# Attention scores from bf16 part stacks, or from float32 operands on row strips of TensorE, in a four-layer gated cross-attention kernel

## The chip, the cores and the metric

The kernel runs on one core of a Trainium2 chip. Its engines work side by side and meet at semaphores: TensorE (PE in the profile; its weight loads are listed apart as PEld), VectorE (DVE), ScalarE (ACT), GpSimd (POOL) and SyncE (SP), which here only issues DMAs. ACT and POOL issue DMAs too. TensorE writes to PSUM, of which the kernel uses eight banks of 128x512 float32; everything else lies in SBUF or in DRAM. The metric is the device time of one execution in microseconds; the median of several runs is compared.

## The reference

Eight batch elements of 256 tokens with 256 features pass four layers. Each layer adds a gated cross-attention and then a gated feed-forward block:

```python
x = x + jnp.tanh(g_xattn[l]) * xattn_l(_layernorm(x), ctx_1024, ...)
x = x + jnp.tanh(g_ffn[l]) * ffn_l(_layernorm(x), ...)
```

Attention has 16 heads of 16 features. Of one layer, with projections and biases (layer 0 has none, its queries, keys and values are the normalised x and the context themselves, and it has a mask over the keys):

```python
scores = jnp.einsum('bqhd,bkhd->bhqk', q, k) / jnp.sqrt(16)
scores = jnp.where(mask == 0, -1e9, scores)          # layer 0 only
attn = jax.nn.softmax(scores, axis=-1)
out = jnp.einsum('bhqk,bkhd->bqhd', attn, v)         # then @ Wo + bo in layers 1 to 3
```

The feed-forward blocks: in layer 0 two dense blocks with GELU over all tokens; in layers 1 and 2 a mixture of eight experts, of which each token takes two; in layer 3 a block with quantized weights and a convolution along the tokens.

## The kernel before, in words

*Order of the work.* The program has three attention runs: one over layers 0 and 1 (the feed-forward of layer 0 and the routing of layer 1 run within it), one over layer 2 (with its routing), one over layer 3 (with its feed-forward). Between them stand the two expert stages, `experts`, with attention's first steps of the next layer woven in. Within a run each head of each element is a unit `u`, 16 to an element (`NH`). For each unit the run emits, in this order: the scores of the units that are due (`scores`), the probabilities of unit `u` (`probs`), every fourth unit the products with the values (`values`), and then whatever was planned for this unit (`plan`). Scores run up to 17 units (`LAG`) ahead of the probabilities, 14 at the start of a run (`FIRST`). TensorE's instructions, ScalarE's exponentials and a few others are pinned to the order in which the code emits them; a scheduler orders the rest, DMA issues included.

*Scores, first pass.* The keys and the queries are held as stacks (`kstack`, `qstack`): three bf16 parts of each number (L196 and L285), laid out as 7 x 16 = 112 rows (`NS`, `NR`, `QP`, `KP`), so that one bf16 product over 112 rows adds the seven products of parts that matter. `scores` (L480) makes two such products of 128 x 256 a head into one PSUM bank, `sc`. VectorE takes the row maximum with its sign turned: in layer 0 with the mask's bias added first (L495), otherwise by a reduction (L500). The maxima go to `nm`.

*From maxima to rows.* After eight heads, `parts` (L504) splits their maxima into three bf16 parts by four VectorE instructions (L198 to L201). `rows` (L515), some units later, transposes them on TensorE (`pn`), copies them to SBUF (`mt`, L526) and sends them by a DMA on ScalarE's queue into rows 112 to 114 of the query stack (L527). The key stacks hold ones in these rows (`ones_of`, L212).

*Scores, second pass.* `probs` (L529) makes the transposed scores, `st`, as two bf16 products over 115 rows, whose last three subtract the maximum. In layer 0 a third product with the bf16 identity adds the mask's bias, 128 x 512 (L542). ScalarE's exponential writes `pT` (L544). `values` (L546) takes four heads at a time: eight float32 products, each onto 32 of the 128 columns of TensorE, into the bank `po`.

*How a stack is made.* In layer 0, `normT` and `contextT` transpose the normalised x and the context on TensorE (`px`, `pc`); later layers project them (`proj`, L414: `pq`, `pk`, two chunks of 128 columns each). `first` (L262) makes the first part on ScalarE (`pc_q`, `pc_k`; L276, L280, L282) and the residual on VectorE (`res_q`, `res_k`; L277, L283). `stack` (L285) makes the second part on VectorE (L295), the third on GpSimd, or on VectorE where it is urgent (L296), writes the three to DRAM (`dr_q`, `dr_k`; L302) and reads them back as the rows of the stack (L309), three or four DMAs each, on SP's queue, in one case shared with ScalarE's.

*Order of features.* For these stacks the features are reordered on the host (`order`, L1558) such that head and feature change places; the context, the weights and the biases are given in this order.

Of the kernel before, what the change touches and what calls it, by code (L numbers as in the profile page):

```python
# [33 lines left out]
QP = (0, 1, 2, 0, 1, 0, 1)  # L34
KP = (0, 1, 0, 1, 2, 2, 0)
# [4 lines left out]
def kernel(ctx: ExitStack, tc: tile.TileContext, a: dict, out: bass.AP):  # L40


# [52 lines left out]
    HC = P // DK  # L95

# [29 lines left out]
    nc.vector.scalar_tensor_tensor(qrow, qrow, -float(TPE), prow, ALU.mult, ALU.add)  # L126

# [53 lines left out]

    NS = len(QP)
    NR = NS * DK
# [10 lines left out]
    def split(dst, src, tmp, engine):  # L196

        engine.tensor_copy(dst[0], src)  # L198
        engine.tensor_tensor(tmp, src, dst[0], ALU.subtract)
        engine.tensor_copy(dst[1], tmp)  # L200
        engine.tensor_tensor(dst[2], tmp, dst[1], ALU.subtract)  # L201


    kkeep = [
        keep.tile([P, HC, DC, S], BF16, tag=f"ks{k}", name=f"kstack_{k}") for k in range(EARLY)
# [6 lines left out]
    def ones_of(engine, ks, va):  # L212

        nc.sync.dma_start(
            ks[NR : NR + 3].rearrange("r h c s -> r (h c s)"), onesb[: 3 * HC * DC * S // P]
        )
        engine.memset(va[:, :, :, DK : DK + 1], 1.0)
        engine.memset(va[:, :, :, DK + 1 :], 0.0)

    def attention(layers):  # L220
# [10 lines left out]
        def setup(l):  # L231
            y = lay[l] = {"bq": None, "bk": None}
            for n in "qkvo":
                w = awpool.tile([P, DC, D], F32, tag=f"w{n}", name=f"w{n}{l}")
                nc.sync.dma_start(w, a[f"L{l}_w{n}"].rearrange("(c p) o -> p c o", p=P))
                y[n] = w

            nc.vector.tensor_scalar(y["q"], y["q"], 1.0 / DK**0.5, None, ALU.mult)
            bv = None
            if l in (1, 3):  # L240
                y["bq"] = load(f"bq{l}", [P, DC], a[f"L{l}_bq"])
                nc.vector.tensor_scalar(y["bq"], y["bq"], 1.0 / DK**0.5, None, ALU.mult)
                y["bk"] = load(f"bk{l}", [P, DC], a[f"L{l}_bk"])
                bv = load(f"bv{l}", [P, DC], a[f"L{l}_bv"])
            y["bo"], y["bv"] = row(f"L{l}_bo"), bv
# [16 lines left out]
        def first(p, s, j, c=None, scale=1.0, bias=None):  # L262

            n = f"{s}{layers[0]}_{j}"
            if not c:
                ops[j, s] = (
                    keep.tile([P, 3, DC * S], BF16, tag="pc", name=f"pc_{n}", bufs=2),
                    keep.tile([P, DC * S], F32, tag="res", name=f"res_{n}", bufs=2),
                )
            pc, r = ops[j, s]  # L270
            cols = slice(0, DC * S) if c is None else slice(c * S, (c + 1) * S)
            pc, r = pc[:, 0, cols], r[:, cols]
            if c is None:
                p = p.rearrange("p c s -> p (c s)")
            if bias is not None:
                nc.scalar.activation(pc, p, AF.Identity, bias=bias)  # L276
                nc.vector.scalar_tensor_tensor(r, p, bias, pc, ALU.add, ALU.subtract)  # L277
                return
            if scale == 1.0:
                nc.scalar.copy(pc, p)  # L280
            else:
                nc.scalar.mul(pc, p, scale)  # L282
            nc.vector.scalar_tensor_tensor(r, p, scale, pc, ALU.mult, ALU.subtract)  # L283

        def stack(s, j, c=None, quick=False):  # L285

            n = f"{s}{layers[0]}_{j}"
            pc, r = ops[j, s]
            st = stacks[s][j % 3]
            if c is not None:  # L290
                cols = slice(c * S, (c + 1) * S)
                pc, r, st = pc[:, :, cols], r[:, cols], st[:, :, c, :]
            else:
                st = st.rearrange("r h c s -> r h (c s)")
            nc.vector.tensor_copy(pc[:, 1], r)  # L295
            (nc.vector if quick else nc.gpsimd).tensor_tensor(pc[:, 2], r, pc[:, 1], ALU.subtract)  # L296

            w = DC * S if c is None else S
            dr = dram.tile([3, P, w], BF16, tag=f"{s}dr{w}", name=f"dr_{n}_{c}", bufs=2)
            engines = [nc.sync] if c is None else [nc.sync, nc.scalar]  # L300
            hold = pin if layers[0] == 0 and j == 0 else lambda d: d
            hold(engines[0].dma_start(dr.rearrange("i p n -> p i n"), pc))  # L302
            rows = dr.rearrange("i (d h) n -> (i d) h n", h=HC)
            part, k = QP if s == "q" else KP, 0
            while k < NS:
                e = k + 1
                while e < NS and part[e] == part[e - 1] + 1:
                    e += 1
                hold(engines[k % len(engines)].dma_start(  # L309
                    st[k * DK : e * DK], rows[part[k] * DK : (part[e - 1] + 1) * DK]  # L310
                ))
                k = e
            return stacks[s][j % 3]

        lead = layers[0] > 0

        def prep(j, l, b):
# [4 lines left out]
            def begin():  # L322
                if l == 0 and j < EARLY:
                    ones_of(nc.vector, stacks["k"][j], vas[j])
                o["nm"] = pool.tile([P, 2, NH], F32, tag="nm", name=f"nm_{n}", bufs=3)

            def ones_own():
                ones_of(nc.gpsimd, stacks["k"][j], vas[j])
# [16 lines left out]
            def contextT():  # L345
# [8 lines left out]
                first(pt, "k", j)  # L354
                o["ks"] = stack("k", j)
                nc.scalar.copy(cT, pt)
                ctxT.append(cT)

            def contextV():
                for i in range(2):  # L360
                    for c in range(DC):
                        nc.gpsimd.tensor_copy(
                            vas[j % 3][:, i, c * HC : (c + 1) * HC, 0:DK],
                            o["cx"][:, i, c * P : (c + 1) * P].rearrange("p (d h) -> p h d", h=HC),
                        )
# [16 lines left out]
            def norm():  # L382
                xn = o["xn"] = work.tile([P, 2, D], F32, tag="xn2", name=f"xn_{n}")
                mv, rs = o["st"]
                for i in range(2):
                    x_, d_ = x[2 * b + i], xn[:, i, :]
                    if l == 0:
                        x_ = x_.rearrange("p (c h d) -> p c d h", c=DC, h=HC)
                        d_ = d_.rearrange("p (c d h) -> p c d h", c=DC, h=HC)
# [9 lines left out]
            def normT():  # L399
                pt = bank(ps_s, "s", f"px_{n}").rearrange("p (c s) -> p c s", c=DC)  # L400
# [6 lines left out]
                if l:  # L407
                    xs = o["xs"] = pool.tile([P, DC, S], F32, tag="xs", name=f"xs_{n}", bufs=1)
                    nc.scalar.copy(xs, pt)
                else:  # L410
                    first(pt, "q", j, scale=1.0 / DK**0.5)
                    o["qs"] = stack("q", j, quick=j < 2)

            def proj(s, oc):  # L414

                if oc == 0:
                    o["p"] = bank(ps_s, "s", f"p{s}_{n}").rearrange("p (c s) -> p c s", c=DC)
                src = o["xs"] if s == "q" else ctxT[b]
                for c in range(DC):
                    mm(  # L420
                        o["p"][:, oc, :], lay[l][s][:, c, oc * P : (oc + 1) * P], src[:, c, :],
                        c == 0, c == DC - 1,
                    )
                bias = lay[l][f"b{s}"]
                begins = s == "q" and lead and j == 0
                if begins or bias is not None and oc:
                    for k in (oc,) if begins else range(DC):
                        first(
                            o["p"][:, k, :], s, j, k,
                            bias=None if bias is None else bias[:, k : k + 1],  # L430
                        )
                elif oc:
                    first(o["p"], s, j)
                if begins:

                    o["qs"] = stack(s, j, oc, True)
                elif oc:
                    o[f"{s}s"] = stack(s, j, quick=s == "q" and lead and j == 1)
# [18 lines left out]
            if l == 0:  # L457
                return own + [
                    (-3, begin), (-3, context), (-3, measure), (-1 + k, norm), (3 + k, normT),
                    (4 + k, contextT), (5 + k, biasT), (6 + k, contextV),  # L460
# [19 lines left out]
        def scores(u):  # L480

            j, h = divmod(u, NH)
            c, hh = divmod(h, HC)
            o = ops[j]
            l = o["l"]
            sc = bank(ps_s, "s", f"sc_{layers[0]}_{u}").rearrange("p (i k) -> p i k", i=2)
            for i in range(2):
                mm(
                    sc[:, i, :], o["qs"][:NR, hh, c, i * P : (i + 1) * P], o["ks"][:NR, hh, c, :],
                    i == 0, i == 1,  # L490
                )
            if l == 0:
                for i in range(2):
# [1134 lines left out]
```

## Time and profile before

| | us |
|---|---|
| median of 3 runs | 1647.01 (1646.47 to 1647.60) |
| the profiled execution's own time | 1639.55 |
| its span, first to last instruction | 1637.6 |

The stages, from the busy times of each stretch:

| stretch (us) | what runs | PE busy | DVE busy | granted clock |
|---|---|---|---|---|
| 0 to 36 | loads, first stacks | 2.4 | 14.3 | 1.00 |
| 36 to 60 | first scores of layer 0 | 11.2 | 18.0 | 0.69 |
| 60 to 560 | attention of layers 0 and 1 | 459.7 | 330.0 | 0.81 to 0.99 |
| 560 to 595 | routing, slots of layer 1 | 20.7 | 25.1 | 0.85 |
| 595 to 860 | experts of layer 1 | 264.0 | 29.9 | 0.99 |
| 860 to 905 | start of layer 2 | 17.2 | 25.9 | 0.66 |
| 905 to 1100 | attention of layer 2 | 170.1 | 161.2 | 0.95 |
| 1100 to 1145 | routing, slots of layer 2 | 30.4 | 32.0 | 0.76 |
| 1145 to 1290 | experts of layer 2 | 137.9 | 43.9 | 0.97 |
| 1290 to 1335 | start of layer 3 | 20.6 | 27.3 | 0.66 |
| 1335 to 1580 | attention and feed-forward of layer 3 | 222.2 | 213.7 | 0.96 |
| 1580 to 1638 | end of the last feed-forward | 38.1 | 35.9 | 0.82 |

How to read it: a line of the profile names the engine, the line of the kernel, the operation and the tiles, out<-in, with the buffer numbers left out. Where a helper such as `mm` (L189) or `turn` (L194) records all products or transposes, all carry its line, so the tiles tell them apart. Matmuls are pipelined and overlap: an instruction of 256 columns in bf16 is listed as 0.27 to 0.28 us long while the next starts 0.11 us later, so "busy" includes tails. A float32 product is listed as two instructions, as the counts show: the eight products of four heads with the values appear as `po` x16.

### The profile page before, as it was taken

The numbers are of one execution on the slowest core, as the hardware profiler recorded it, in microseconds if no ns is written. First come the engines' busy times: TensorE is split into PE (matmuls) and PEld (weight loads), VectorE is DVE, ScalarE is ACT, GpSimd is POOL, SyncE is SP. The second block draws the span as 40 slices with busy tenths as digits, with TensorE's granted clock in tenths as the row PEclk, the third lists the DMA queues.
The fourth block names the chain that finished last, engine by engine and source line by source line (L and its number), as shares of the span: only waits on it lengthen the run. The fifth ranks groups of instructions, "written<-read, shape, count | busy, mean of one in ns | idle before, by whom it ended". The sixth has DMA issues, their size and how long they took to land.

```text
span 1637.6 us, 27767 instructions
## 1 busy us (share of the span) xinstructions
PE 1394.5 (85%) x10002; PEld 1087.7 (66%) x10002; DVE 957.2 (58%) x3131; ACT 725.5 (44%) x1652; POOL 431.1 (26%) x487
## 2 busy tenths in 40 slices
PE   1499999999988969999993798886899758999986
PEld 1357777777665659999992565554899535666765
DVE  4775665555787731111115788976152277899975
ACT  1265555555555523333320554551233225676773
POOL 1322111112211043443324333101554433221000
PEclk9699999999999979999996999987999879999997
DMA  6754332224354061324226545403624344343100
GB/s 180 170 159 101 92 85 66 66 66 120 90 119 106 21 200 48 136 91 145 91 85 187 128 127 124 123 15 84 220 84 160 90 110 101 79 110 92 38 8 20
DMA packets 99808, 169.38 MB, mean 103 GB/s; under 512 B 24754, under 2 KB 84021, under 8 KB 88885
## 3 DMA queue, kind: packets, MB, share of 16 engines
q1 hardware_dynamic: 70943, 116.81, 27.4%
q0 software_dynamic: 22080, 48.61, 9.4%
q10 hardware_dynamic: 6646, 2.15, 0.7%
q8 instruction: 81, 1.33, 0.3%
q14 instruction: 58, 0.48, 0.1%
HBM read 217.07 MB, written 41.68 MB: 158 GB/s over the span
## 4 chain that ended last, share of the span: by engine, by line
PE 58%; DVE 27%; DMA 7%; POOL 3%; issue 2%; ACT 2%; SPq 0%; POOLq 0%; ACTq 0%; DVEq 0%
PE phg L189 12%; PE yg L189 11%; DVE nm L500 6%; PE y_f L189 4%; PE po L189 4%; PE ph_f L189 4%; PE st L189 4%; PE sc L189 3%; PE pk L189 2%; DMA qstack<-mt 2%; PE pq L189 2%; PE py L189 2%; DVE h_f L1404 2%; DVE ms L495 2%; PE cv_f L189 1%
## 5 line engine op out<-in xcount | busy, mean ns | idle before, releaser
L544 ACT ACTIVATE pT<-st 128x512 f32<-128x512 f32 x512 | 295.8, 601 | 211.1 <-PE st L189 201.2
L500 DVE TENSOR_REDUCE nm<-sc 128x2 f32<-128x512 f32 x384 | 257.0, 681 | 58.9 <-PE sc L189 57.9
L189 PE MATMUL sc<-kstack,qstack 112*128 112x256 bf16 x1024 | 203.8, 288 | 59.5 <-DMA kstack<-dr_k_None 27.6
L189 PE MATMUL st<-qstack,kstack 115*128 115x256 bf16 x1024 | 199.6, 279 | 25.1 <-DMA qstack<-mt 16.5
L189 PEld LDWEIGHTS <-qstack 112*128 112x128 bf16 x1024 | 99.1, 104 | 119.9 <-issue 57.3
L1164 ACT ACTIVATE hg<-phg,we 128x128 f32<-128x128 f32 x296 | 84.4, 368 | 184.3 <-issue 165.7
L189 PE MATMUL po<-pT,va 128*32 128x256 f32 x2048 | 147.5, 403 | 7.3 <-DVE nm L500 7.3
L189 PEld LDWEIGHTS phg<-xgT,we 128*128 128x128 f32 x1184 | 140.0, 192 | 4.2 <-issue 0.9
L189 PE MATMUL phg<-xgT,we 128*128 128x128 f32 x1184 | 140.7, 275 | 1.1 <-issue 0.6
L189 PE MATMUL yg<-we,hg 128*128 128x256 f32 x592 | 136.1, 379 | 0.0
L189 PEld LDWEIGHTS <-kstack 115*128 115x128 bf16 x1024 | 100.7, 100 | 48.5 <-DMA qstack<-mt 17.5
L495 DVE CUSTOM_DVE_ANT_0 ms<-sc,mb 128x256 f32<-128x256 f32 x256 | 107.4, 419 | 39.8 <-PE sc L189 30.6
L189 PEld LDWEIGHTS yg<-we,hg 128*128 128x128 f32 x592 | 108.7, 190 | 12.7
L167 POOL TENSOR_TENSOR rsr_ff<-rsv_ff,nhalf 128x4 f32<-128x4 f32 (+1 forms) x32 | 28.5, 889 | 322.9 <-DVE rsv_ff L161 167.8
L189 PEld LDWEIGHTS po<-pT,va 128*32 128x32 f32 x2048 | 56.0, 113 | 66.2 <-issue 25.8
L1144 DVE COPY xgT<-ptg 128x256 f32<-128x256 f32 x36 | 15.3, 424 | 127.5 <-PE ptg L194 127.5
L1177 DVE TENSOR_TENSOR ysb<-yg,we 128x256 f32<-128x256 f32 x51 | 21.6, 424 | 104.4 <-PE yg L189 101.4
L296 POOL TENSOR_TENSOR pc_k<-res_k,pc_k 128x512 bf16<-128x512 f32 x32 | 37.1, 1159 | 153.5 <-DVE pc_k L295 126.5
L1083 POOL DMA_INDIRECT xg<-xd,toki x72 | 69.0, 958 | 23.1 <-issue 22.5
L1083 POOL DMA_INDIRECT yg<-yd,rt_si x64 | 63.3, 988 | 43.2 <-issue 16.2
L1164 ACT ACTIVATE hg<-phg,w 128x128 f32<-128x128 f32 x136 | 38.8, 368 | 78.4 <-issue 68.2
L560 ACT COPY oS<-po 128x256 f32<-128x256 f32 x128 | 48.0, 375 | 57.0 <-PE po L189 35.9
(260 smaller groups left out, 2706.9 us busy)
## 6 DMA issues: line engine op xcount, KB each, us to landing
qstack<-dr_q_None SPq DMA_DIRECT2D x60, 256.0 KB
dr_k_None<-pc_k SPq DMA_DIRECT2D x32, 384.0 KB
kstack<-dr_k_None SPq DMA_DIRECT2D x32, 384.0 KB
dr_q_None<-pc_q SPq DMA_DIRECT2D x30, 384.0 KB
qstack<-dr_q_None SPq DMA_DIRECT2D x30, 384.0 KB
yd<-ysb SPq DMA_DIRECT2D x72, 128.0 KB
kstack<-dr_k_None SPq DMA_DIRECT2D x32, 256.0 KB
kstack<-dr_k_None SPq DMA_DIRECT2D x64, 128.0 KB
```

What stands on the lines that cost most here:

```text
L167: pw = nc.gpsimd.tensor_tensor(rs, ve, nhalf[:, :k, :n], ALU.pow)
L189: pin(nc.tensor.matmul(out, lhsT=lhsT, rhs=rhs, start=start, stop=stop, skip_group_check=True))
L296: (nc.vector if quick else nc.gpsimd).tensor_tensor(pc[:, 2], r, pc[:, 1], ALU.subtract)
L495: nc.vector.tensor_tensor_reduce(masked, sc[:, i, :], o["bias"][:, i, :], -1.0, 3.0e38, ALU.add, ALU.min, o["nm"][:, i, h : h + 1],)
L500: nm = nc.vector.tensor_reduce(o["nm"][:, :, h], sc, AX.X, ALU.max, negate=True)
L544: pin(nc.scalar.activation(pT[u], st, AF.Exp))
L560: nc.scalar.copy(oS[j][:, g, :], po.pop(j)[:, 0, :])
L1083: return nc.gpsimd.indirect_dma_start(out=dst, out_offset=None, in_=src, in_offset=bass.IndirectOffsetOnAxis(ap=rows, axis=0), **kw,)
L1144: nc.vector.tensor_copy(xT, pv)
L1164: nc.scalar.activation(h[:, hc, :], ph[:, k, :], AF.Gelu, bias=w[:, n1 - nh + hc : n1 - nh + hc + 1],)
L1177: nc.vector.tensor_tensor(ys, py, w[:, nh * D :], ALU.add)
L1404: nc.vector.scalar_tensor_tensor(y, hp[:, k, t : t + S], cw[:, hc, t : t + 1], y, ALU.mult, ALU.add)
```

## The change

Queries and keys stay in float32, unsplit. Each head's 16 features lie on the first 16 of a strip of 32 rows, four heads to a tile of 128 rows, four such chunks (`CH`). Row 16 of each strip holds the negated maximum in the queries and a one in the keys.

- `scores` and `probs` take two heads at a time, on neighbouring strips; their four products alternate between the two strips. They run on even units only.
- `parts` is gone; `rows` transposes the float32 maxima as they are. `column` says in which order the maxima lie.
- `first`, `stack`, `split` and the DRAM buffers are gone, and with them the part DMAs.
- In layers 1 to 3, Wq and Wk are padded on the host to 512 columns, 16 features and 16 zeros a head; `proj` makes four chunks in two banks, and ScalarE evicts them straight into queries and keys. The ones of the keys come with the bias (`orow`).
- In layer 0, `norm` writes into padded tiles (`xp`), and `pads` transposes these, and for the keys the padded values `va` (which hold the ones), into queries and keys. `contextV` is moved ahead and goes to VectorE for the first two elements. `pT` has eight buffers instead of six.

```diff
-            for i in range(2):
-                mm(
-                    sc[:, i, :], o["qs"][:NR, hh, c, i * P : (i + 1) * P], o["ks"][:NR, hh, c, :],
-                    i == 0, i == 1,
-                )
+            for i in range(2):
+                for k in range(2):
+                    rows = slice(32 * (h0 % 4 + k), 32 * (h0 % 4 + k) + DK)
+                    mm(
+                        sc[k][:, i, :], o["qs"][rows, c, i * P : (i + 1) * P], o["ks"][rows, c, :],
+                        i == 0, i == 1,
+                    )
...
-                mm(
-                    st[:, i, :], o["ks"][: NR + 3, hh, c, i * P : (i + 1) * P],
-                    o["qs"][: NR + 3, hh, c, :], i == 0, l > 0 and i == 1,
-                )
-            if l == 0:
-                mm(st, identb, o["biasT"], False, True)
+                for k in range(2):
+                    rows = slice(32 * (h0 % 4 + k), 32 * (h0 % 4 + k) + DK + 1)
+                    mm(
+                        st[k][:, i, :], o["ks"][rows, c, i * P : (i + 1) * P], o["qs"][rows, c, :],
+                        i == 0, l > 0 and i == 1,
+                    )
+            for k in range(2):
+                if l == 0:
+                    mm(st[k], identb, o["biasT"], False, True)
...
-            pn = bank(ps_s, "s", f"pn_{n}").bitcast(BF16)[: 3 * HC, :S]
+            pn = bank(ps_s, "s", f"pn_{n}")[:HC, :S]
...
+                turn(pn[:, i * P : (i + 1) * P], o["nm"][:, i, c * HC : (c + 1) * HC], ident)
-            nc.scalar.dma_start(o["qs"][NR : NR + 3, :, c, :], mt)
+            nc.scalar.dma_start(o["qs"][DK::32, 2 * c : 2 * c + 2, :], mt)
...
+            def pads(src, dst, scale, name):
+                for h in range(2):
+                    pt = bank(ps_s, "s", f"p{name}_{n}_{h}").rearrange("p (c s) -> p c s", c=2)
+                    for c in range(2):
+                        for i in range(2):
+                            k = 4 * (2 * h + c)
+                            turn(
+                                pt[:, c, i * P : (i + 1) * P],
+                                src[:, i, k : k + 4, :].rearrange("p h d -> p (h d)"), ident,
+                            )
+                    if scale == 1.0:
+                        nc.scalar.copy(dst[:, 2 * h : 2 * h + 2, :], pt)
+                    else:
+                        nc.scalar.mul(dst[:, 2 * h : 2 * h + 2, :], pt, scale)
...
             def contextV():
                 for i in range(2):
-                    for c in range(DC):
-                        nc.gpsimd.tensor_copy(
...
+                    (nc.vector if j < EARLY else nc.gpsimd).tensor_copy(
+                        vas[j % 3][:, i, :, 0:DK],
+                        o["cx"][:, i, :].rearrange("p (h d) -> p h d", d=DK),
+                    )
...
+            def proj(s, h):
+                p = bank(ps_s, "s", f"p{s}_{n}_{h}").rearrange("p (c s) -> p c s", c=2)
+                dst = o[f"{s}s"] = stacks[s][j % 3]
+                src = o["xs"] if s == "q" else ctxT[b]
+                for k in range(2):
+                    lo = (2 * h + k) * P
+                    for c in range(DC):
+                        mm(
+                            p[:, k, :], lay[l][s][:, c, lo : lo + P], src[:, c, :],
+                            c == 0, c == DC - 1,
+                        )
+                scale, bias = 1.0 / DK**0.5 if s == "q" else 1.0, lay[l][f"b{s}"]
+                if bias is not None:
+                    for k in range(2):
+                        nc.scalar.activation(
+                            dst[:, 2 * h + k, :], p[:, k, :], AF.Identity,
+                            bias=bias[:, 2 * h + k : 2 * h + k + 1], scale=scale,
+                        )
+                elif s == "k":
+                    nc.scalar.activation(dst[:, 2 * h : 2 * h + 2, :], p, AF.Identity, bias=orow)
                 else:
-                    first(pt, "q", j, scale=1.0 / DK**0.5)
-                    o["qs"] = stack("q", j, quick=j < 2)
...
+                    nc.scalar.mul(dst[:, 2 * h : 2 * h + 2, :], p, scale)
...
-                plan(at, parts, j, c)
-                plan(at + (3 - (c == 0) if j == 0 else 4), rows, j, c)
+                plan(at + (1 if j == 0 else 2), rows, j, c)
...
                 for i in ahead_of.get(u, ()):
-                    scores(i)
-                if 0 <= u < NU:
+                    if i % 2 == 1:
+                        scores(i - 1)
+                if 0 <= u < NU and u % 2 == 0:
                     probs(u)
```

## The prediction

> **What bounds the kernel now.** I read the page's busy times and its chain that ended last, then the busy times of each stretch, then the TensorE timeline inside one steady stretch, then the chain at the start.
>
> ```profile
> PE 1394.5 (85%) x10002; PEld 1087.7 (66%) x10002; DVE 957.2 (58%) x3131; ACT 725.5 (44%) x1652; POOL 431.1 (26%) x487
> PE 58%; DVE 27%; DMA 7%; POOL 3%; issue 2%; ACT 2%; SPq 0%; POOLq 0%; ACTq 0%; DVEq 0%
> ```
>
> TensorE carries most of the chain. An average over stages can mislead, so here are the five stretches in which attention runs (start:end, length, then busy time of PE, PEld, DVE, ACT, POOL, granted clock, DMA share, GB/s).
>
> ```profile
> 60.00:110.00 50.00, 38.38 (x297) 21.79 (x296) 37.59 (x171) 23.32 (x46) 14.38 (x17) 0.81 0.72 181
> 110.00:400.00 290.00, 279.21 (x1910) 210.48 (x1910) 169.42 (x672) 158.47 (x305) 54.93 (x70) 0.99 0.33 82
> 400.00:560.00 160.00, 142.08 (x1202) 98.25 (x1194) 123.02 (x418) 89.59 (x198) 21.72 (x24) 0.97 0.38 97
> 905.00:1100.00 195.00, 170.09 (x1386) 115.77 (x1384) 161.24 (x515) 104.33 (x220) 48.56 (x52) 0.95 0.42 105
> 1335.00:1580.00 245.00, 222.21 (x1767) 160.27 (x1767) 213.70 (x547) 166.35 (x336) 47.42 (x50) 0.96 0.31 78
> ```
>
> In the longest, PE is busy 279.2 of 290.0 us and DVE 169.4. Only in the last does DVE come near, 213.7 beside 222.2 of 245.0. PE's idle time over the five is 11.6+10.8+17.9+24.9+22.8 = 88 us. The timeline of layer 0 shows what fills it; the distance from one line's start to the next is what its instructions cost.
>
> ```profile
> 240.41 0.38 PE L189 MATMUL st<-qstack,kstack 115*128 115x256 bf16 x2
> 240.63 0.38 PE L189 MATMUL st<-mbT,identb 128*128 128x512 bf16 x1
> 240.94 1.07 PE L189 MATMUL po<-pT,va 128*32 128x256 f32 x16
> 241.94 0.66 PE L194 MATMUL acc<-ident,oS 128*128 128x128 f32 x4
> 242.43 0.38 PE L189 MATMUL sc<-kstack,qstack 112*128 112x256 bf16 x2
> ...
> 245.15 0.69 PE L189 MATMUL pgb<-row_L_bo,ones 1*128 1x256 f32 x2
> 245.77 0.39 PE L189 MATMUL sc<-kstack,qstack 112*128 112x256 bf16 x2
> ...
> 255.32 1.02 PE L189 MATMUL pq<-xs,wq 128*128 128x256 f32 x4
> 256.18 0.38 PE L189 MATMUL sc<-kstack,qstack 112*128 112x256 bf16 x2
> ```
>
> Prices: a bf16 product of 256 columns 0.22/2 = 0.11 us. A float32 product appears as two instructions (`pq` has four for two products), each 0.86/4 = 0.215 us. A float32 transpose 0.49/4 = 0.12 us. `po` works on four strips of 32 columns: 16 instructions in 1.00 us, 0.0625 each, so four run side by side. Around a change of strip shape there is a pause: `po` starts 0.31 after a 0.22 us product, 0.09 late, and its 1.00 us are four rounds of 0.216 and some 0.1; the one-row `pgb`, which also uses a strip, takes 0.62 for two instructions, 0.43 of work and two pauses of 0.09.
>
> ```profile
> 606.82 3.46 PE yg L189 x16
> 610.27 3.57 PE phg L189 x32
> ```
>
> The chain in the expert stage confirms it: 3.46/16 = 0.216 us per float32 instruction of 256 columns, 3.57/32 = 0.112 with 128 columns and a float32 weight load each. So a weight load costs at most 0.112 when loads follow each other.
>
> **The change part by part.** All is summed onto the profiled execution's span, 1637.6 us.
>
> *Scores, both passes.* Before: `sc` x1024 and `st` x1024 in bf16, 2048 x 0.11 = 225 us. After: the same products in float32, two instructions each, 4096. Bounds of one instruction: 0.216 if the strips take turns (`yg`), 0.0625 if four run side by side (`po`). The change has two heads on two strips of 32 rows, so I take 0.216/2 = 0.108, and 0.11 with starts, beside `phg`'s 0.112 where loads set the pace: 451 us, +226. Ends: +31 and +660. This lies on PE, the bound, with nothing to hide it.
>
> One rule speaks against even that. The Trainium skill, "TensorE: Matmul & The Clock Gate", Part 3 ("What overlaps and what doesn't"), says that matmuls start and end strictly in program order. The two instructions of one float32 product stand together and share a strip, so by it a set of eight would need five rounds, not four, and the total would come to about 1988 us. The row of `po` disagrees: in that order its 16 would need nine rounds, 1.9 us, and it took 1.00, so I follow the row.
>
> *Projections.* Wq and Wk are padded to 512 columns: `pq` and `pk` go from 192 instructions each to 384. 384 x 0.216 = +83 us on PE.
>
> *Transposes.* In layer 0 `px` has 8 an element instead of 4 and the keys take 8 more: 96 x 0.12 = +12 us.
>
> *Changes of strip shape.* Counted in the built programs: 384 before, 732 after, as every run of scores now lies between full-size work (layer 0's mask product follows each pair). 348 x 0.09 = +31 us; 0 if the pauses hide, the upper end counted below.
>
> PE's sum: +226+83+12+31 = +352 us.
>
> *What PE's idle time takes up.* Added PE work can use the time in which PE waited for others. I take the 88 us of the table. Lower end 0, if the same waits come later. Upper end 171 us: a busy PE counts each product's tail of 0.16 us (0.38 long at 0.22 apart); counting the five stretches' instructions at the prices above instead leaves 19+24+33+47+48 free.
>
> *Removed from other engines.* DVE loses the residuals (L277 30.7 and L283 21.2 us), casts (L295 27.6), quick third parts (L296 4.4) and the maxima's parts (L198 to L201, 49.2): 133 us. POOL loses 58 third parts, 68.6 us, and 20 of 32 copies into `va`. SP loses 293 DMAs, most of queue 1's 116.8 MB. These are worth nothing beyond the 88 us above, as PE covers them; were DVE the bound in 1335:1580, its share would shorten that stretch, but PE's added work there exceeds it.
>
> *Added on ACT.* Projections and transposes are now evicted straight into keys and queries: 128 of 128x256 (L276's 473 ns) and 64 of 128x512 (L280's 590) make 98 us, for 48.6 removed. PE hides the 50: in 1335:1580 ACT is busy 166 of 245. Without that cover they cost 50.
>
> *The start.*
>
> ```profile
> 18.03 2.64 DMA dr_q_None<-pc_q
> ...
> 22.12 6.78 DMA dr_k_None<-pc_k
> ...
> 30.22 5.95 DMA kstack<-dr_k_None
> 36.42 3.14 PE sc L189 x14
> ...
> 51.72 5.60 DMA qstack<-mt
> ```
>
> The trip by DRAM between 15 and 36.4 us goes, 21 us at most. Instead 24 transposes and two copies of 0.6 stand there, some 5 us. New waits: layer 0's copies into `va` move to DVE for the first two elements; those of element 1 stand ahead of the first maximum and need `cx`, which SP now issues behind twelve loads of x and three weights, 2.8 MB, some 11 us at the 250 to 270 GB/s of 20 to 40 us. All maxima queue behind that wait, and the first `st` behind them. Between 0 and -21, I take -15. The row transfer of 5.6 us stays. The starts of layers 2 and 3 lose a smaller trip (in layer 2 `pq` ends at 880.4, `sc` begins at 890.5) but pay double projections at half clock and still wait for `yg` (885.9 to 893.8): -5 each, from -10 to 0.
>
> *Sum.* 1637.6 + 352 - 88 - 15 - 10 = 1877 us. The profiled run timed 1639.6 and the three runs have a median of 1647.0, 9.4 above the span; so 1886 us.
>
> **The rivals.**
>
> *The strips take turns.* For it: the two instructions of a product share a strip, and no row of before has row strips side by side. Against it: `po`. 4096 x 0.216 = 885 us, +434 over mine: 2320 us.
>
> *Faster: four strips side by side.* If the scores of one pair ran beside the probabilities of another on the other two strips, 4096 x 0.0625 = 256 us, 195 less: 1691; if PE also used all 171 idle us, 1608, faster. The price at which it decides: with 171 taken up, PE's sum must fall by 156, to 0.11 - 156/4096 = 0.072 us an instruction. Against it: scores run 16 heads ahead, and 16 is a multiple of 4, so at each step scores and probabilities use the same two strips; the 732 changes leave only some two sets in a run; and weight loads at 0.112 would hold it if they are one stream.
>
> *Banks.* A pair opens two of eight PSUM banks at once, which DVE empties at 681 ns a head (L500). If each of the 192 pairs of layers 1 to 3 waits for one such read, 192 x 0.68 = +130: 2016 us. Against it: PE's own time per pair grows past 2 us, DVE's shrinks.
>
> **How the numbers follow.** Forecast 0.80, strips in turn 0.08, four side by side 0.06 (half of it faster at all, with a mere grain at no change), banks 0.06. Some 0.2% is what a measurement of this kernel can tell from no change. Low end: 171 us taken up and no pauses, 1886-83-31 = 1772. High end: nothing taken up, and a pause of 0.09 before each of 512 sets, 1886+88+46 = 2020, which takes in the banks. So 1770 to 2020; faster 0.05, same 0.01, slower 0.94.
>
> **What would show it.** After: `sc` and `st` with 2048 instructions each, 16 or 17 rows, in sets of eight some 0.88 us long; `pq` and `pk` 384 each; PE near 0.97 busy in attention; the expert stages unchanged at about 265 and 145 us; the first `sc` near 20 us. Sets of 1.7 us mean strips in turn; sets of 0.45 us, four side by side; long waits of `sc` for the maximum's reduction, banks. I am wrong if PE's idle time in attention stays as it is, or if the sum on PE is not what lengthens the stretches.

## The result, and the profile after

The changed kernel takes 2006.94 us (median of four, 2001.75 to 2015.97) against 1646.74 us (four, 1644.35 to 1647.60): a ratio of 1.2196, 95% interval 1.2146 to 1.2246. The profiled execution took 2001.75 us, with a span of 2000.0.

The page after, busy times and the chain that ended last:

```profile
PE 1886.7 (94%) x12530; PEld 1421.1 (71%) x12530; DVE 880.6 (44%) x2711; ACT 769.4 (38%) x1747; POOL 354.3 (18%) x411
PE 83%; DVE 9%; DMA 3%; issue 2%; POOL 2%; ACT 1%; another core or an unknown queue 0%; POOLq 0%; SPq 0%; ACTq 0%; DVEq 0%
```

TensorE's share of the chain went from 58% to 83%; VectorE has less to do, and its share of the chain fell from 27% to 9%. The stretches with attention (start:end, length, then busy time of PE, PEld, DVE, ACT, POOL, granted clock, DMA share, GB/s):

```profile
50.00:100.00 50.00, 49.65 (x296) 28.79 (x296) 19.50 (x89) 16.26 (x33) 0.80 (x2) 0.66 0.06 16
100.00:400.00 300.00, 298.65 (x1958) 212.98 (x1956) 124.94 (x528) 127.83 (x250) 25.54 (x36) 0.93 0.02 6
400.00:700.00 300.00, 297.87 (x2032) 212.71 (x2030) 134.01 (x366) 124.00 (x266) 21.62 (x29) 0.89 0.05 18
...
1080.00:1390.00 310.00, 305.51 (x2004) 205.12 (x2002) 158.14 (x460) 114.60 (x237) 36.43 (x41) 0.79 0.06 19
...
1610.00:1950.00 340.00, 332.61 (x2381) 238.45 (x2380) 208.04 (x465) 181.67 (x366) 32.45 (x39) 0.89 0.04 12
```

Two things are to be seen. TensorE has hardly any idle time left here. And the clock, 0.95 to 0.99 in the long attention stretches before, is 0.79 to 0.93, lowest (0.66) in a stretch where TensorE is busy for 49.65 of 50 us.

A steady stretch of layer 2 in the timeline (start, length, then engine, line, operation and tiles):

```profile
1202.13 1.13 PE L188 MATMUL sc<-keys,qs 16*128 16x256 f32 x8
1203.10 1.03 PE L188 MATMUL st<-qs,ks 17*128 17x256 f32 x8
1204.06 1.99 PE L188 MATMUL pq<-xs,wq 128*128 128x256 f32 x8
1205.99 1.13 PE L188 MATMUL sc<-keys,qs 16*128 16x256 f32 x8
```

From one start to the next, eight instructions of a pair take 0.97 us and eight full-size ones 1.93: on strips two run at once, as priced.

To compare kernels, the rest of the text splits a span in three. TensorE's busy time on the page is divided by the trace's records of the granted clock (one value for each 3.4 us, 1 or 0.5). Busy time at half clock counts half as work and half as lost; what is not busy is idle. The records begin at 41.6 us in the kernel before and at 18.3 us after; what TensorE did until then, 7.5 and 5.3 us, counts as full clock, although the transposes there take 0.213 us each and later ones 0.109. The 1.00 of the first stretch in the table of before is no measurement either.

| kernel (us) | span | work at full clock | lost at half clock | TensorE idle |
|---|---|---|---|---|
| before | 1637.6 | 1325.4 | 69.1 | 243.1 |
| after | 2000.0 | 1667.6 | 219.0 | 113.3 |
| difference | +362.4 | +342.2 | +149.9 | -129.8 |

### The profile page after: what moved, and what is told of

Its sections match the earlier page's. It is cut to its first block, busy times and chain, and to the rows that moved or that the text cites. A ratio compares the mean times of both kernels' runs of the same rounds, so it can differ in the third digit from the quotient of the medians.

```text
span 2000.0 us, 31689 instructions
## 1 busy us (share of the span) xinstructions
PE 1886.7 (94%) x12530; PEld 1421.1 (71%) x12530; DVE 880.6 (44%) x2711; ACT 769.4 (38%) x1747; POOL 354.3 (18%) x411
## 4 chain that ended last, share of the span: by engine, by line
PE 83%; DVE 9%; DMA 3%; issue 2%; POOL 2%; ACT 1%; another core or an unknown queue 0%; POOLq 0%; SPq 0%; ACTq 0%; DVEq 0%
PE st L188 13%; PE sc L188 13%; PE yg L188 9%; PE phg L188 9%; PE po L188 7%; PE pq L188 5%; PE pk L188 4%; PE y_f L188 4%; PE ph_f L188 4%; PE py L188 3%; PE pv L188 2%; PE acc L193 1%; PE cv_f L188 1%; PE px L193 1%; DVE nm L465 1%
## 5 line engine op out<-in xcount | busy, mean ns | idle before, releaser
L188 PE MATMUL sc<-keys,qs 16*128 16x256 f32 x1472 | 243.8, 468 | 1.0 <-DVE nm L465 0.9
L188 PE MATMUL st<-qs,keys 17*128 17x256 f32 x1472 | 225.6, 427 | 0.4 <-DVE nm L460 0.4
L188 PEld LDWEIGHTS sc<-keys,qs 16*128 16x128 f32 x1472 | 146.7, 219 | 64.8 <-issue 33.7
L188 PEld LDWEIGHTS st<-qs,keys 17*128 17x128 f32 x1472 | 160.2, 211 | 31.2 <-issue 4.3
L188 PE MATMUL pq<-xs,wq 128*128 128x256 f32 x384 | 117.7, 462 | 1.4 <-ACT xs L369 1.4
L188 PEld LDWEIGHTS pq<-xs,wq 128*128 128x128 f32 x384 | 85.3, 232 | 30.5 <-issue 9.5
L188 PE MATMUL pk<-ctxT,wk 128*128 128x256 f32 x384 | 93.7, 395 | 2.2 <-DVEq L1188 2.0
L188 PE MATMUL st<-qs,ks 17*128 17x256 f32 x576 | 90.3, 429 | 0.7 <-DVE nm L460 0.7
L188 PE MATMUL sc<-ks,qs 16*128 16x256 f32 x576 | 86.3, 419 | 0.0
L188 PEld LDWEIGHTS pk<-ctxT,wk 128*128 128x128 f32 x384 | 72.9, 196 | 17.8 <-issue 5.5
```

The lines of the kernel that those rows point to most:

```text
L188: pin(nc.tensor.matmul(out, lhsT=lhsT, rhs=rhs, start=start, stop=stop, skip_group_check=True))
```

## The experiments

Each was profiled once, except the last two, which were also timed in several rounds. The kernel before took 1646.4 us beside the first four, 1647.0 beside the next four, 1636.3 beside the three after these and 1636.4 beside the last; differences between groups of some 10 us say nothing.

**32 rows in a strip.** Both passes of the changed kernel read whole strips; the added rows hold zeros.

```diff
-                    rows = slice(32 * (h0 % 4 + k), 32 * (h0 % 4 + k) + DK)
+                    rows = slice(32 * (h0 % 4 + k), 32 * (h0 % 4 + k) + 32)
...
-                    rows = slice(32 * (h0 % 4 + k), 32 * (h0 % 4 + k) + DK + 1)
+                    rows = slice(32 * (h0 % 4 + k), 32 * (h0 % 4 + k) + 32)
```

> Both passes of the scores read all 32 rows of a strip instead of 16 and 17; the added rows hold zeros (in the first pass row 16 holds a zero in the queries and a one in the keys), so the scores are the same. Theory: what the sum missed is the granted clock, which stood at one half during 438 us of busy TensorE in the changed kernel (138 us in the one before) because the strips use few of the 128 rows; with twice the rows the mean clock rises from 0.88 to 0.92 or more and the time falls from 2007 to 1880 to 1950 us, the sets of eight staying at four rounds of 0.21 us at full clock. Rival: the clock falls for another reason, the number of rows (or of zeros) plays no part: mean clock 0.87 to 0.89, time 1995 to 2020 us.

Measured: 1877.96 us, 129 less than after and 2 below the theory's range; mean clock 0.951. Work 1680.3, lost 72.8, idle 123.0. The same stretches of this kernel:

```profile
50.00:100.00 50.00, 49.67 (x428) 31.60 (x426) 32.91 (x148) 22.98 (x47) 4.07 (x6) 1.00 0.05 13
100.00:400.00 300.00, 297.87 (x2017) 216.97 (x2016) 123.93 (x497) 135.21 (x265) 26.95 (x38) 0.98 0.02 6
```

From 50 to 100 TensorE is as busy as after, but at a clock of 1.00 in place of 0.66 it gets through 428 instructions in place of 296. The number of instructions, their order and their results are the same. So the clock answers to the rows that an instruction uses, zeros or not.

**Four strips.** A pair's scores and another pair's probabilities, two steps apart (`LAG` 19), are issued in turn on four strips.

```diff
+            beside, done = probs(later, True) if later is not None else (lambda i: None, lambda: None)
             for i in range(2):
                 for k in range(2):
...
+                beside(i)
+            done()
```

> Scores run two heads further ahead (LAG 19), so that the pair of scores and the pair of probabilities of one step lie on different strips, and their eight products are emitted in turn. Theory: strips run side by side, four as well as two, so that 16 instructions take four rounds of 0.21 us instead of eight: the price of 4096 instructions falls from 451 to 221 us at full clock, half as many strip runs stay as they are, and the time falls to 1700 to 1800 us, lower still if the clock stays up with more rows in use. Rival: two at a time is the limit (weight loads of 0.11 us each follow one another, 16 x 0.11 = 1.8 us): 1980 to 2020 us.

Measured: 1867.14 us, above the theory's 1700 to 1800 and far below the rival's 1980. Work 1542.4, 125 less than after; lost 174.6; idle 148.2. Its timeline in layer 2:

```profile
1130.73 0.48 PE L188 MATMUL sc<-keys,qs 16*128 16x256 f32 x2
1130.74 0.55 PE L188 MATMUL st<-qs,keys 17*128 17x256 f32 x2
1131.05 0.38 PE L188 MATMUL sc<-keys,qs 16*128 16x256 f32 x2
1131.07 0.45 PE L188 MATMUL st<-qs,keys 17*128 17x256 f32 x2
1131.27 0.38 PE L188 MATMUL sc<-keys,qs 16*128 16x256 f32 x2
1131.28 0.45 PE L188 MATMUL st<-qs,keys 17*128 17x256 f32 x2
1131.48 0.38 PE L188 MATMUL sc<-keys,qs 16*128 16x256 f32 x2
1131.50 0.45 PE L188 MATMUL st<-qs,keys 17*128 17x256 f32 x2
1131.87 1.07 PE L188 MATMUL po<-pT,va 128*32 128x256 f32 x16
```

Two scores and two probabilities start within 0.02 us; sixteen instructions take four rounds, 1.14 us to the next start, where after takes 0.97 + 0.96. Four strips do run side by side. Most of the gain in time is the work; 174.6 us are still lost to the clock, beside 219.0.

**The projections twice.** The kernel before, with each product of queries and keys with their weights made twice.

```diff
-                for c in range(DC):
+                for c in 2 * tuple(range(DC)):
```

> The kernel before, with the products of the q and k projections made twice into the same bank: 384 more instructions of 0.216 us, 83 us of TensorE, and nothing else of the change. It prices the projections' term and what TensorE's idle time takes up. Theory of the prediction: added TensorE work first fills idle time; the idle time near these projections takes up a third to a half, so the time goes from 1647 to 1685 to 1705 us. Rival: idle time takes up nothing, all 83 us are paid: 1725 to 1735 us. Other rival: all of it hides, 1645 to 1660 us.

Measured: 1704.97 us, 58.6 more than the kernel before beside it. Work 1406.2, lost 67.9, idle 229.1: 80.8 of work were added, where the prediction's 384 x 0.216 is 83. Idle time took up 14 of it, less than the third to a half that was expected.

**bfloat16 on the strips.** The changed kernel with queries, keys and maxima of the strips rounded to bfloat16, so that each product is one instruction.

```diff
-            mt = pool.tile([HC, S], F32, tag="mt", name=f"mt_{n}", bufs=3)
+            mt = pool.tile([HC, S], BF16, tag="mt", name=f"mt_{n}", bufs=3)
...
-            return pool.tile([P, CH, S], F32, tag=f"{s}s{k}", name=f"{s}s{layers[0]}_{k}", bufs=1)
+            return pool.tile([P, CH, S], BF16, tag=f"{s}s{k}", name=f"{s}s{layers[0]}_{k}", bufs=1)
```

> Queries, keys and the rows of maxima are kept in bf16, so each product is one instruction of 0.11 us instead of two of 0.216; the layout on strips, the projections, transposes and changes of strip shape stay (the scores are those of rounded queries and keys, so the output differs from the reference). Theory: the float32 passes are what costs; the sets of eight become sets of four in two rounds of 0.11, 2048 x 0.055 = 113 us instead of 451, and the time falls by some 340 us and the clock's share to 1600 to 1690 us. Rival: the strips themselves cost (changes of shape, loads, a low clock whatever the type): 1750 us or more.

Measured: 1641.88 us, as the theory had it, beside 1646.39 for the kernel before. Work 1350.1, lost 109.4, idle 180.6. Float32 on strips instead of bfloat16 is 317.5 us of work; by the prediction's prices it would be 4096 x 0.11 - 2048 x 0.055 = 338.

**Four strips of 32 rows.** The edits of the first two experiments together.

> The changed kernel with a pair's scores and another pair's probabilities issued in turn on four strips, and with 32 rows (the added ones zeros) in every strip. Theory 1, the two gains are separate (the clock follows the rows in use, and the first strips leave the other half of the array idle): 32 rows alone brought 129 us (2007 to 1878) and four strips alone 140 (2007 to 1867), so together near 1740, with a granted clock of 0.94 or more. Theory 2, both gains are the clock's, one gain taken twice: near 1860, clock near 0.95. Theory 3, four strips of 32 rows are as much work for the array as full products, and with the idle time gone the clock stays high: 1650 to 1700.

Measured: 1822.5 us, clock 0.936. Work 1557.2, lost 97.0, idle 166.5. No theory's number: four strips take work off (123 us beside 32 rows alone) and rows take lost time off (78 us beside four strips alone), so the gains are separate in kind, but 53 us more than after are idle, and 97 us stay lost.

**Four heads of 32 rows.** `scores` and `probs` take four heads at once.

```diff
-                for k in range(2):
-                    rows = slice(32 * (h0 % 4 + k), 32 * (h0 % 4 + k) + DK)
+                for k in range(4):
+                    rows = slice(32 * (h0 % 4 + k), 32 * (h0 % 4 + k) + 32)
...
-                    if i % 2 == 1:
-                        scores(i - 1)
-                if 0 <= u < NU and u % 2 == 0:
+                    if i % 4 == 3:
+                        scores(i - 3)
+                if 0 <= u < NU and u % 4 == 0:
```

> The changed kernel with four heads side by side in each pass (the scores of four heads, then the probabilities of four heads, half as often) and 32 rows in every strip. Beside the kernel with two heads and 32 rows (1878) it runs the same instructions, twice as many at once, and the changes of the strips' shape go from 732 to about half. Theory 1: four at once halve the rounds, so that some 220 us of TensorE's time go, of which other engines' work gives back up to half, and the changes saved bring about 35 (174 of 0.2 us): 1640 to 1760. Theory 2, that only two strips are ever in work at a time: near 1845, the changes alone.

Measured: 1817.1 us, between the two theories. Work 1516.7, lost 96.8, idle 201.9. The changes of shape counted in the traces are 681, against 732 with two heads: the expectation's "about half" was wrong, as projections and values still lie between the sets. The work fell by 164 against two heads with 32 rows, and half of that, 79, came back as idle time.

**Head by head.** All products of one head, then all of the other.

```diff
-            for i in range(2):
-                for k in range(2):
+            for k in range(2):
+                for i in range(2):
```

> The changed kernel with the instructions of a pair in another order: all four products of head A, then all four of head B, in place of A and B in turn. Theory 1, instructions start in the program's order and only those next to each other overlap: a set of 8 takes 7 rounds of 0.21 in place of 4, so 0.63 us more on each of 512 sets, 320 us in all, near 2330. Theory 2, an instruction for a free strip starts past those that wait for a busy one: 4 rounds as before, near 2007, in the trace pairs of starts a few ns apart on both strips.

Measured: 2010.32 us, as after and as theory 2 had it. Its timeline:

```profile
1214.73 1.14 PE L188 MATMUL sc<-keys,qs 16*128 16x256 f32 x8
1215.70 1.13 PE L188 MATMUL st<-qs,ks 17*128 17x256 f32 x8
```

Eight instructions in 0.97 us again, four of one strip issued ahead of four of the other. So an instruction for a free strip started past at least three that waited for a busy one.

**bfloat16 with 32 rows.** The edits of the first and the fourth experiment together.

> The changed kernel with queries, keys and row maxima of the strips rounded to bfloat16, and 32 rows in each strip: each product one instruction in place of two. Beside the float32 kernel with 32 rows (1878 us, clock 0.951) it shows what the second pass of float32 costs where the clock is high in both; beside the bfloat16 kernel with 16 rows (1642 us, clock 0.917) what the rows bring there. Theory 1, rows and passes are separate terms: half clock in busy time was 219 us there against 438, so the rows bring about 129 x (219-138)/(438-138), near 35 us: 1600 to 1615, and the float32 passes cost about 270 us at equal clock. Theory 2, the clock's part belongs to float32: the rows bring nothing, 1642.

Measured: 1636.16 us. Work 1352.2, lost 98.2, idle 183.9. The rows bring 11 us of lost time here against 146 in float32. The gain was less than theory 1's 35: most of the loss is still there.

**24 rows, and 32 in the first pass alone.** By then the traces had shown a rule for the clock (last section). These two tested it; the edits are those of the first experiment, with 24 in place of 32 in both passes, and with the first of the two lines alone.

> The changed kernel with 24 rows in every strip of both passes, halfway between 16 or 17 (2007 us, clock 0.881) and 32 (1878, clock 0.951); added rows are zeros. Theory 1, taken from the nine runs so far: TensorE's share of cells at work (rows in use x columns in use x time, over its 128x128) in one 3.4 us record of the clock sets the next record, half below 38%, full above; that describes 97% of their records. By it the clock lies between: records under 38% are 68 of 544 with the strips' part of the 32-row trace scaled to 24 rows, some 20 more that stay low once low, against 54 and 140 in the two traces: clock 0.92 to 0.94, 1905 to 1940 us. Theory 2, a strip must be full to count: near 2007, clock 0.88. Theory 3, some 20 rows a strip are enough: near 1878.

> The changed kernel with 32 rows in the first pass's strips alone, 17 in the second's, so that as many cells are at work in all as with 24 rows in both. Theory 1 (share of cells at work in a record sets the next record's clock): the same as with 24 rows within some 20 us, clock 0.92 to 0.94. Theory 2 (only full strips count): between, 1930 to 1950, while 24 rows stay near 2007.

Measured: 1901.72 us (clock 0.934; work 1676.7, lost 102.8, idle 120.5) and 1899.59 us (0.939; 1679.0, 94.8, 124.0). The first is 3 us below theory 1's range and far from theory 2's 2007; the second lies within 2 us of the first, as theory 1 has it, and 30 below theory 2's range. The kernel before was 10 us faster beside these two than beside the earlier ones, which is too little to change this. A strip need not be full to count.

The kernel with 24 rows, the same stretches:

```profile
50.00:100.00 50.00, 49.68 (x425) 31.83 (x424) 32.27 (x145) 22.77 (x47) 4.07 (x6) 0.99 0.05 15
100.00:400.00 300.00, 297.87 (x2034) 216.25 (x2032) 123.24 (x493) 135.59 (x267) 26.93 (x38) 0.98 0.02 5
```

Seven or eight rows more in each strip bring the clock from 0.66 to 0.99 in the first of these.

**bfloat16, four heads, 32 rows.**

> The bfloat16 kernel with 32 rows (1636 us) with four heads side by side in both passes; queries, keys and maxima of the strips are rounded to bfloat16. Theory 1: TensorE's time at full clock falls by half of 2048 x 0.054 (55 us) and by 174 changes of shape of 0.2 (35), and as from two to four heads in float32 half of it comes back as idle time (there 163 of work gone, 79 of idle time more): near 1590, faster than before by 3%. Theory 2: VectorE, busy 846 and close to TensorE in layer 3, takes over and nothing is won: 1625 to 1645.

Measured, three rounds: 1679.92 us against 1636.25, ratio 1.0288 (1.0257 to 1.0319). Slower than before, against both theories. Work fell by 42 to 1310.4, but idle time grew from 183.9 to 267.4. TensorE's waits, first with two heads, then with four (engine, line, what it waited for: total, times, longest):

```profile
PE pt_f L193 <- DVE fxn_f L1330: 10.4, 4, 5.0
...
PE pn L193 <- DVE nm L465: 5.8, 5, 2.2
```

```profile
PE pt_f L193 <- DVE fxn_f L1330: 23.9, 8, 5.8
PE pn L193 <- DVE nm L465: 17.5, 8, 4.9
PE pn L193 <- DVE nm L460: 17.1, 16, 5.6
PE pm L193 <- ACT pT L501: 16.9, 11, 1.5
...
PE pq L188 <- ACT xs L369: 12.2, 19, 1.2
```

Four heads hand VectorE four maxima and ScalarE four exponentials in one burst, and TensorE's next small steps (`pn`, `pm`) stand behind these in order. That this burst is the cause is read from the waits, not tried by itself.

**The faster one, timed.**

> The bfloat16 kernel with two heads and 32 rows again (queries, keys and maxima of the strips rounded to bfloat16), timed beside the kernel before on one chip, as it is the only one that has come below it (1636.2 beside 1647.0 in one look each). Theory 1, the gain is real: 0.4 to 0.9% faster. Theory 2, it is the spread of single executions: within 0.3%.

Measured, five rounds: 1627.93 us (1623.0 to 1632.6) against 1636.40, ratio 0.9943 (0.9924 to 0.9962). The gain is real and small, and it belongs to a kernel that rounds what the changed one keeps in float32.

## Why the prediction was right, and where it was off

The direction, the place (TensorE in attention) and most sizes held; the time lies in the range, 121 us above the forecast. Against the sum's 1877 us of span, measured 2000.0:

- *TensorE's sum*, +352: measured +342.2 of work. The work can be shared out by tile, each instruction counted from its start to the next one's start or to its own end, at full clock. Then `sc` and `st` without the mask went from 254.5 to 482.4 us, +228 where +226 was forecast; `pq`, `pk` and `px` (layer 0's key transposes are listed as `pk` too) brought +101, forecast 83 + 12; all else +13. The third experiment put the projections at 80.8, and the bfloat16 experiments the float32 pass at 318 to 328, against 338 by the same prices. That the scores' term came out is partly luck: both sides lay some 30 us above their price (225 and 451), and in the difference this cancels. After, a set takes 0.97 us, not 0.88. Single starts show why: at 1202.14 us the first scores start 0.09 late behind full-size work, and their second round comes 0.31 us later in place of 0.21. So a change of shape costs some 0.2 us. The prediction saw both delays in the row of `po` and priced the first alone. Its +31 for the changes has no tile of its own and is spread over these figures.
- *Idle time taken up*, -88, with -15 and -10 for the starts: -113 in all. Measured: idle time -129.8, over the whole span. The "upper end 171" was not reached.
- *The start*, -15: the first `st` came at 57.4 us before and at 40.15 after, 17 earlier. The wait that the prediction named is in the chain at the start:

```profile
13.70 4.47 DMA wq<-in_L_wq
...
18.25 4.41 DMA cx<-in_ctx
22.69 0.50 DVE va L317 x2
23.19 0.33 DVE ms L460
```

The copies of element 1 wait for `cx`, which came behind x and the weights, and the first maximum stands behind them.

- *The clock*, not a term at all: measured +149.9. This is the step that failed. "I take 0.216/2 = 0.108, and 0.11 with starts" used rows at a clock near 1.0, and carried them over as if the clock would stay; the only clock in the sum was that of the starts of layers 2 and 3. It makes up the miss: 9.8 less work than +352, 16.8 more idle time taken up than 113, and 149.9 of lost time, +123 in all. The experiment with 32 rows shows it by itself: it gives 129 us back although the work grew by 13, because the lost time fell from 219.0 to 72.8. That the range held the time was luck: its upper end was made of idle time not taken up and of pauses, and neither is what came.

Of the rivals, *the strips take turns* is refuted by sets of 0.97 us. *Four side by side* did not happen between scores and probabilities, as the same two strips are used at each step. It did where several pairs of scores follow each other, as at the start:

```profile
18.18 2.05 PE L188 MATMUL sc<-keys,qs 16*128 16x256 f32 x24
```

These are some 0.08 us an instruction, below the 0.108 of two strips. The experiment with four strips shows that it can be had at most steps, and there it is worth 125 us of work rather than the 195 priced. *Banks*: scores waited for the maximum's reduction for 0.9 us in all, so they cost nothing:

```profile
L188 PE MATMUL sc<-keys,qs 16*128 16x256 f32 x1472 | 243.8, 468 | 1.0 <-DVE nm L465 0.9
L188 PE MATMUL st<-qs,keys 17*128 17x256 f32 x1472 | 225.6, 427 | 0.4 <-DVE nm L460 0.4
```

(busy, mean ns, then the idle time before and what ended it). The prediction set aside the rule of the Trainium skill, "TensorE: Matmul & The Clock Gate", Part 3 ("What overlaps and what doesn't"), that matmuls start strictly in program order. Head by head, that rule would have cost some 320 us, and the kernel took 3 more than after: the measurement decides, for instructions on different strips.

## What to carry to other kernels

A price per instruction holds at the clock of the row that it came from: before carrying it into a stage with other instructions, ask how much of the 128x128 array that stage keeps at work, not how busy TensorE is. Instructions on half-filled strips can lose half the clock while TensorE never pauses; zeros in the spare rows gave 129 of 2007 us back. And work taken off TensorE comes back as waits once VectorE and ScalarE are asked for more at once: 79 of 164 us with four heads in float32, more than all of it in bfloat16.

## What the runs showed of the clock

The Trainium skill, "TensorE: Matmul & The Clock Gate", Part 1 ("What's actually happening"), says that the clock is gated by how busy TensorE has been. Here busy is not enough. After, TensorE is never idle in this stretch:

```profile
61.00:72.00 11.00, 11.00 (x60) 5.34 (x60) 3.52 (x18) 3.20 (x7) 0.00 (x0) 0.61 0.01 2
72.00:83.00 11.00, 11.00 (x56) 5.80 (x56) 4.31 (x19) 3.33 (x7) 0.00 (x0) 0.54 0.02 3
```

What fits is the share of the array's cells at work. Give each matrix instruction the rows times the columns of its weights, times its duration at full clock (0.107 us for 256 bfloat16 columns, 0.215 for a float32 instruction of 256), spread evenly from its start, over twice the time at half clock. Add these up over one 3.4 us record of the clock, and divide by 128 x 128 x 3.4 us. A share under 38% goes with half clock in the *next* record, a share above it with full clock. Over the traces of before, after and eleven experiments (all but the timed repeat), 116 of 6802 records contradict this, 1.7%; of the two that were made to test it, 8 of 552 and 9 of 551. Simpler quantities do worse, each with the threshold that suits it best: rows times time without the columns is wrong in 243 records, the instructions' time alone in 596, TensorE's busy time in 665. "Always full clock" would be wrong in 1086. The trace of before alone has 3 of 468 against the rule, so it could have been read there.

By this rule it is plain why float32 pairs suffer: two strips of 16 rows use 32 of 128 rows, 25%; of 24 rows, 37.5%; of 32 rows, 50%. And by it the low clock holds itself: at half clock even the full array comes to no more than 50%. In layer 0 of the kernel after (start of the record, its clock, its share):

```
195.81  1.0  30%
199.23  0.5  21%
202.64  0.5  30%
206.05  0.5  26%
209.47  0.5  17%
212.88  0.5  41%
216.29  1.0 100%
```

TensorE's timeline over the same time:

```profile
204.52 2.08 PE L188 MATMUL sc<-keys,qs 16*128 16x256 f32 x8
206.39 1.92 PE L188 MATMUL st<-qs,keys 17*128 17x256 f32 x8
208.24 1.03 PE L188 MATMUL st<-mbT,identb 128*128 128x512 bf16 x2
209.06 1.06 PE L193 MATMUL pt_f<-ident,fxn_f 128*128 128x128 f32 x4
210.05 2.08 PE L188 MATMUL sc<-ks,qs 16*128 16x256 f32 x8
211.92 1.92 PE L188 MATMUL st<-qs,keys 17*128 17x256 f32 x8
213.77 1.03 PE L188 MATMUL st<-mbT,identb 128*128 128x512 bf16 x2
214.59 1.87 PE L193 MATMUL px<-ident,xp 128*128 128x128 f32 x8
216.30 4.05 PE L188 MATMUL ph_f<-xT_f,w 128*128 128x256 f32 x18
```

The strips' sets take 1.87 us here, nearly twice the 0.97 of the earlier rows, with no gap between them; only when the full-size mask product and transposes fill most of a record does the clock come back. The share is reckoned, and 38% fitted, from these traces; that it is the quantity the chip itself watches was not shown, only that it describes these records better than the three simpler ones, and that rows of zeros, 24 rows, and rows in one pass alone all move the clock as it says.
